# The mixture of LoRA experts of a four-block kernel, rewritten as a pipeline over tiles

## The chip, the cores and the metric

The kernel runs on one core of a Trainium2 chip. The time is device microseconds of that core for one execution. The text speaks of the engines as the profile does: PE is TensorE's matmul, PEld its weight load, DVE is VectorE, ACT is ScalarE, POOL is GpSimd, SP is SyncE, which here only starts DMAs.

## What is computed

The whole kernel is four blocks, each an attention-like mixer and a feed-forward part, on x of 16 x 128 x 256 in fp32. Only the last feed-forward part, a mixture of eight LoRA experts of rank 64, is changed. Of the reference, this part:

```python
def _L3_ffn_ref(x, A, B, Wr, br):          # x after layer norm
    x_flat = x.reshape(-1, d)
    logits = (x_flat @ Wr.T + br) / TEMPERATURE
    probs = jax.nn.softmax(logits, axis=-1)
    expert_idx = jnp.argmax(probs, axis=-1)
    expert_weight = jnp.max(probs, axis=-1)
    h = jnp.einsum('nd,erd->ner', x_flat, A)
    y = jnp.einsum('ner,eor->neo', h, B) * SCALING          # SCALING = 1/64
    sel = jnp.take_along_axis(y, expert_idx[:, None, None], axis=1)[:, 0, :]
    return sel * expert_weight[:, None]
...
x = x + jnp.tanh(g_ffn[3]) * _L3_ffn_ref(_layernorm(x, axis=-1), L3_ffn_A, L3_ffn_B, L3_ffn_Wr, L3_ffn_br)
```

The kernel doesn't gather: it computes the hidden row of all eight experts (512 numbers per token), multiplies it with a gate that is zero for seven of them, and takes the product with all of B.

## The kernel before, in words

A tile is one of the 16 blocks of 128 tokens (128 x 256); x lies in SBUF throughout, in four tensors xg[0..3] of GB = 4 tiles each, a group. The program is the function `passage`; it is followed by a second one under `tc.If`, which runs only when a flag says that a softmax sum left a safe range. In this execution it doesn't run. The flag is made by `verdict` (lines 66 to 80) from running extremes `inv`: four small DVE operations, a matmul with a column of ones (L76), three DVE operations on its result. All engines read the flag at the end (L48).

The stage ahead, `stage_l3x` (lines 1495 to 1801), is an attention whose order on PE, DVE and ACT is written out by hand (`tc.manual_schedule` over these three engines): instructions stay in the order in which the Python emits them. It ends, tile by tile, with `keep_values` (avs, L1704), `back` (ta, L1709), `normalise` (rc, inv, o: L1716, L63, L64, L1719), `turn` (tt, L1724), `keep_turned` (oT, L1729), `output` (y, L1735) and `store` (ys on ACT, L1740, and x on POOL, L1742).

The stage of the change is `stage_l3f` (lines 1804 to 1843). It is not under a manual schedule, so a scheduler orders its instructions; it also moved the group's layer norm statistics (`layernorm`, L155 to L160) of most groups into the attention. The loop runs over the four groups:
- layer norm of the group (xn, L163, with the power -0.5 on POOL, L160), `transposed` (L166 to L174: 8 transposes in two halves, copied out by DVE and ACT, L173), `logits` (L345, two fp32 matmuls of 8 columns a tile) and `exp_shifted` (L355).
- the gate: sum, reciprocal, `topk_mask` (L325 to L339, six DVE operations, four of them on 128 x 256 numbers) and three products (L1814 to L1819).
- for each tile of the group: ph = xn A (L1823, two fp32 matmuls with 512 columns), hid = ph times gate (L1831, DVE), four transposes of hid (L1835, tile tp), a copy to SBUF on ACT (hT, L1837), y = hid B (L1840, four fp32 matmuls with 256 columns), and x = x + tanh(g) y (L1842, DVE).
- one store of the group's four tiles, 512 KB (L1843, SP queue).

Each fp32 matmul shows in the trace as two passes, each with its weight load; a transpose is one. PSUM has two buffers for each of ph, y and tp. `verdict` is called between the two stages and has a PSUM pool of its own.

Other stages of the kernel (the shared expert of the first block, from line 516) are already written as pipelines in the manner that the change brings here; `stats` and `normal` of that stage (L593 to L605) are nearly the same functions.

Of the kernel before, what the change touches and what calls it, by code (L numbers as in the profile page):

```python
# [22 lines left out]
GB = 4  # L23
E = 8
I = 176
EI = E * I
LN_EPS = 1e-5
# [28 lines left out]
def passage(ctx: ExitStack, tc: tile.TileContext, a: dict, out: bass.AP, inv, flag):  # L56
    nc = tc.nc
    search = inv is None
# [4 lines left out]
            nc.vector.tensor_tensor(inv[:, 0, n], inv[:, 0, n], rc, ALU.max)  # L63
            nc.vector.tensor_tensor(inv[:, 1, n], inv[:, 1, n], rc, ALU.min)  # L64

    def verdict():

        with tc.tile_pool(name="vd", bufs=1) as vd, tc.tile_pool(name="vdp", bufs=1, space=PSUM) as ps:
            m = vd.tile([P, 2, 2], F32, name="m")
            nc.vector.tensor_reduce(m[:, 0], inv[:, 0], AX.X, ALU.max)  # L70
            nc.vector.tensor_reduce(m[:, 1], inv[:, 1], AX.X, ALU.min)
            nc.vector.tensor_scalar(m[:, 0], m[:, 0], 1e20, None, ALU.is_gt)
            nc.vector.tensor_scalar(m[:, 1], m[:, 1], 1e-30, None, ALU.is_lt)
            m = m.rearrange("p a b -> p (a b)")
# [16 lines left out]
    xg = [cst.tile([P, GB, D], F32, name=f"x{g}") for g in range(NG)]  # L91
# [15 lines left out]
    tri = consts[:, 7:71]  # L107
    sel = consts[0:2, 71:199]

    tg = cst.tile([P, 8], F32, name="tg")  # L110
# [4 lines left out]
    neghalf = cst.tile([P, GB], F32, name="neghalf")  # L115
# [33 lines left out]
    def layernorm(pool, g, extra=None, tag="xn"):  # L149

        x = xg[g]
        st = small.tile([P, GB, 6], F32, name="st")
        mv = small.tile([P, GB, 2], F32, name="mv")
        for k in range(GB):
            nc.vector.bn_stats(st[:, k, :], x[:, k, :])  # L155
            nc.vector.bn_aggr(mv[:, k, :], st[:, k, :])
        ve = small.tile([P, GB], F32, name="ve")
        nc.vector.tensor_scalar_add(ve, mv[:, :, 1], LN_EPS)
        rs = small.tile([P, GB], F32, name="rs")
        nc.gpsimd.tensor_tensor(rs, ve, neghalf, ALU.pow)  # L160
        xn = pool.tile([P, GB, D], F32, name="xn", tag=tag)
        for k in range(GB):
            nc.vector.tensor_scalar(xn[:, k, :], x[:, k, :], mv[:, k, 0:1], rs[:, k : k + 1], ALU.subtract, ALU.mult)  # L163
        return xn

    def transposed(pool, ps, xn, tag="xnT"):  # L166

        xT = pool.tile([P, 2, GB * P], F32, name="xnT", tag=tag)
        for c in range(2):
            t = ps.tile([P, GB * P], F32, name="tp", tag="tp")  # L170
            for k in range(GB):
                nc.tensor.transpose(t[:, k * P : (k + 1) * P], xn[:, k, c * P : (c + 1) * P], ident)
            (nc.scalar.copy if c else nc.vector.tensor_copy)(xT[:, c, :], t)  # L173
        return xT  # L174
# [35 lines left out]
    def stage_l0x(ka, vbuf, anyk):  # L210

        with tc.tile_pool(name="s0", bufs=1) as s0, tc.tile_pool(name="s0w", bufs=2) as s0w, tc.tile_pool(
# [103 lines left out]
            for b in range(0, B, 2):  # L316
# [3 lines left out]
                        nc.tensor.transpose(t[:, (2 * k + c) * P : (2 * k + c + 1) * P], oT[:, c, b + k, :], ident)  # L320
                xv = xg[b // GB][:, b % GB : b % GB + 2, :].rearrange("p b d -> p (b d)")
                nc.vector.scalar_tensor_tensor(xv, t, tg[:, 0:1], xv, ALU.mult, ALU.add)


    def topk_mask(v, k, pool):  # L325

        n = v.shape[1]
        mine, other = bc(v, 3, E), bc(v, 2, E)
        gt = pool.tile([P, n, E, E], F32, name="gt", bufs=1)
        nc.vector.tensor_tensor(gt, other, mine, ALU.is_gt)  # L330
        eq = pool.tile([P, n, E, E], F32, name="eq", bufs=1)
        nc.vector.tensor_tensor(eq, other, mine, ALU.is_equal)
        f = "p t a b -> p t (a b)"
        nc.vector.tensor_tensor(eq.rearrange(f), eq.rearrange(f), bc(tri, 1, n), ALU.mult)
        nc.vector.tensor_tensor(gt.rearrange(f), gt.rearrange(f), eq.rearrange(f), ALU.add)
        m = pool.tile([P, n, E], F32, name="m")
        nc.vector.tensor_reduce(m, gt, AX.X, ALU.add)
        nc.vector.tensor_scalar(m, m, k - 0.5, None, ALU.is_lt)
        return m  # L339

    def logits(ps, xT, gw, bias=None):
        lg = ps.tile([P, GB, E], F32, name="lg", tag="tp")
        for k in range(GB):
            for c in range(2):
                nc.tensor.matmul(  # L345
                    lg[:, k, :], lhsT=xT[:, c, k * P : (k + 1) * P], rhs=gw[:, c, :], start=(c == 0), stop=(c == 1)
                )
        l = small.tile([P, GB, E], F32, name="l")
        if bias is None:
            nc.vector.tensor_copy(l, lg)  # L350
        else:
            nc.vector.tensor_tensor(l, lg, bc(bias, 1, GB), ALU.add)
        return l

    def exp_shifted(l):  # L355

        mx = small.tile([P, GB], F32, name="mx")
        nc.vector.tensor_reduce(mx, l, AX.X, ALU.max)
        ex = small.tile([P, GB, E], F32, name="ex")
        nc.vector.tensor_tensor(ex, l, bc(mx, 2, E), ALU.subtract)  # L360
        nc.scalar.activation(ex, ex, AF.Exp)
        return ex


    def moe0_weights():
# [1436 lines left out]


    def stage_l3f(wa, wb, wr, br):
        with tc.tile_pool(name="lo", bufs=2) as lo, tc.tile_pool(name="lot", bufs=2, space=PSUM) as pst, tc.tile_pool(
            name="lou", bufs=2, space=PSUM
        ) as psu:
            for g in range(NG):
                xn = layernorm(lo, g)
                xT = transposed(lo, pst, xn)  # L1810
                ex = exp_shifted(logits(pst, xT, wr, br))

                s = small.tile([P, GB], F32, name="s")
                nc.vector.tensor_reduce(s, ex, AX.X, ALU.add)  # L1814
                nc.vector.reciprocal(s, s)
                gate = small.tile([P, GB, E], F32, name="gate")
                nc.vector.tensor_tensor(gate, ex, topk_mask(ex, 1, lo), ALU.mult)
                nc.vector.tensor_tensor(gate, gate, bc(s, 2, E), ALU.mult)
                nc.vector.tensor_scalar(gate, gate, 1.0 / 64.0, None, ALU.mult)  # L1819
                for k in range(GB):  # L1820
                    ph = psu.tile([P, E, 64], F32, name="ph")
                    for c in range(2):
                        nc.tensor.matmul(  # L1823
                            ph.rearrange("p e r -> p (e r)"),
                            lhsT=xT[:, c, k * P : (k + 1) * P],
                            rhs=wa[:, c, :],
                            start=(c == 0),
                            stop=(c == 1),
                        )
                    hid = lo.tile([P, E, 64], F32, name="hid")  # L1830
                    nc.vector.tensor_tensor(hid, ph, bc(gate[:, k, :], 2, 64), ALU.mult)  # L1831
                    t = pst.tile([P, 4, P], F32, name="tp")
                    hf = hid.rearrange("p e r -> p (e r)")
                    for i in range(4):
                        nc.tensor.transpose(t[:, i, :], hf[:, i * P : (i + 1) * P], ident)  # L1835
                    hT = lo.tile([P, 4, P], F32, name="hT")
                    nc.scalar.copy(hT, t)  # L1837
                    y = psu.tile([P, D], F32, name="y")
                    for i in range(4):
                        nc.tensor.matmul(y, lhsT=hT[:, i, :], rhs=wb[:, i, :], start=(i == 0), stop=(i == 3))  # L1840
                    xv = xg[g][:, k, :]
                    nc.vector.scalar_tensor_tensor(xv, y, tg[:, 7:8], xv, ALU.mult, ALU.add)  # L1842
                nc.sync.dma_start(out[g * GB : (g + 1) * GB].rearrange("b p d -> p b d"), xg[g])  # L1843

# [138 lines left out]
```

## Time and profile before

| what | us |
|---|---|
| median of 3 runs (1096.06 to 1099.82) | 1098.37 |
| the profiled execution | 1106.34 |
| its span, from the first to the last instruction | 1104.5 |
| first transpose of the stage starts | 999.66 |
| last x update of the stage ends | 1098.03 |
| mean granted TensorE clock of the span | 0.906 |

The profile is of one execution. A group of instructions is named by line, engine and operation, as out<-in by the tiles' names; busy matmuls overlap, so that their starts say more than their lengths. The granted clock is TensorE's, as a share of full speed. Of the whole span PE is busy 82%, DVE 56%, ACT 39%, POOL 33%; the stage of the change takes about the last tenth of it.

### The profile page before, as it was taken

The numbers are of one execution on the slowest core, as the hardware profiler recorded it, in microseconds if no ns is written. First come the engines' busy times: TensorE is split into PE (matmuls) and PEld (weight loads), VectorE is DVE, ScalarE is ACT, GpSimd is POOL, SyncE is SP. The second block draws the span as 40 slices with busy tenths as digits, with TensorE's granted clock in tenths as the row PEclk, the third lists the DMA queues.
The fourth block names the chain that finished last, engine by engine and source line by source line (L and its number), as shares of the span: only waits on it lengthen the run. The fifth ranks groups of instructions, "written<-read, shape, count | busy, mean of one in ns | idle before, by whom it ended". The sixth has DMA issues, their size and how long they took to land.

```text
span 1104.5 us, 14954 instructions
## 1 busy us (share of the span) xinstructions
PE 909.0 (82%) x5212; PEld 597.7 (54%) x5212; DVE 614.9 (56%) x1524; ACT 432.8 (39%) x658; POOL 365.9 (33%) x415
## 2 busy tenths in 40 slices
PE   3899888899999999966642858998179899998886
PEld 1444466677777454424422747887145555555563
DVE  5988947222225466349979677453445555545432
ACT  1211033232322444436750243455267677881110
POOL 5766222533024233045420136550533433200000
PEclk9999989999999999989985558899579999997999
DMA  9100080234313119000000202353589776610010
GB/s 304 34 0 0 3 232 1 77 100 108 70 58 124 34 39 187 1 0 1 1 1 0 77 1 77 115 146 85 154 230 252 199 209 191 174 44 1 20 39 22
DMA packets 71322, 94.12 MB, mean 85 GB/s; under 512 B 9191, under 2 KB 63047, under 8 KB 68935
## 3 DMA queue, kind: packets, MB, share of 16 engines
q1 hardware_dynamic: 56872, 67.21, 20.5%
q0 software_dynamic: 14080, 23.78, 10.8%
q10 hardware_dynamic: 288, 2.10, 0.5%
q8 instruction: 45, 0.74, 0.3%
q14 instruction: 37, 0.30, 0.1%
HBM read 57.06 MB, written 33.55 MB: 82 GB/s over the span
## 4 chain that ended last, share of the span: by engine, by line
PE 57%; DVE 21%; issue 8%; POOL 6%; ACT 5%; DMA 2%; another core or an unknown queue 0%; ACTq 0%; POOLq 0%; SPq 0%; DVEq 0%
PE y L307 8%; PE ub L674 4%; PE av L1693 3%; PE yb L700 3%; POOL yc L767 3%; PE s L1142 3%; PE y L1840 3%; PE s L1677 3%; PE yb L970 3%; PE av L1151 3%; PE up L535 2%; PE tq L1100 2%; DVE xn L163 2%; PE ph L1823 2%; DVE inp L489 1%
## 5 line engine op out<-in xcount | busy, mean ns | idle before, releaser
L1684 ACT ACTIVATE pt<-s 128x1024 f32<-128x1024 f32 x128 | 126.3, 1023 | 36.9 <-PE s L1677 34.4
L767 POOL DMA_INDIRECT yc<-ys,pos x64 | 62.0, 968 | 129.1 <-DVE x L786 55.2
L307 PE MATMUL y<-kv,toep 128*128 128x512 f32 x192 | 86.7, 603 | 1.1 <-DVE toep L247 1.1
L1677 PE MATMUL s<-qa,ka 64*128 64x256 f32 x512 | 64.3, 331 | 7.8 <-ACT pt L1684 7.0
L299 POOL TENSOR_TENSOR kv<-ctxT 128x1024 f32<-128x1024 f32 x32 | 60.1, 1899 | 28.5 <-PE y L307 28.5
L1693 PE MATMUL av<-pt,v 128*32 128x256 f32 x1024 | 69.4, 389 | 0.1
L1677 PEld LDWEIGHTS s<-qa,ka 64*128 64x128 f32 x512 | 38.5, 187 | 46.4 <-issue 22.9
L307 PEld LDWEIGHTS y<-kv,toep 128*128 128x128 f32 x192 | 35.6, 192 | 43.2 <-issue 39.8
L674 PE MATMUL ub<-L0we,xbT 128*128 x160 | 52.4, 472 | 2.6 <-ACT xbT L665 2.6
L651 POOL DMA_INDIRECT xb<-xs,who x40 | 38.1, 952 | 45.2 <-PE tb L663 34.2
L970 PE MATMUL yb<-L2we,hT 88*128 (+1 forms) x224 | 42.2, 318 | 8.3 <-DVE hT L794 4.0
L155 DVE BATCH_NORM_STATS2 st<-x 128x6 f32<-128x256 f32 x48 | 19.7, 415 | 52.3 <-POOL x L1742 39.8
L905 POOL DMA_INDIRECT xb<-xs,who x40 | 38.1, 952 | 30.4 <-PE tb L917 20.7
L1584 POOL TENSOR_TENSOR hl<-f,hl 128x512 fp32r<-128x512 f32 x16 | 20.5, 1281 | 77.9 <-ACT hl L1583 77.9
L312 DVE TENSOR_TENSOR pr<-y,qT 128x1024 f32<-128x1024 f32 x32 | 39.0, 1221 | 12.3 <-PE y L307 9.4
L1704 DVE COPY avs<-av 128x256 f32<-128x256 f32 x64 | 26.7, 417 | 30.9 <-PE av L1693 30.9
L535 PE MATMUL up<-L0s,xT 128*128 128x352 f32 x128 | 42.9, 480 | 0.0
L1145 ACT ACTIVATE pt<-s 128x1024 f32<-128x1024 f32 x32 | 32.7, 1023 | 25.4 <-PE s L1142 25.3
L970 PEld LDWEIGHTS yb<-L2we,hT 88*128 88x128 f32 x224 | 34.2, 208 | 15.1 <-DVE hT L794 8.5
L315 DVE TENSOR_REDUCE oT<-pr 128x128 f32<-128x1024 f32 x32 | 38.9, 1219 | 1.0
L674 PEld LDWEIGHTS ub<-L0we,xbT 128*128 128x128 f32 x160 | 29.7, 196 | 16.3 <-ACT xbT L665 2.8
L1693 PEld LDWEIGHTS av<-pt,v 128*32 128x32 f32 x1024 | 26.9, 110 | 20.4 <-issue 0.7
(380 smaller groups left out, 2061.7 us busy)
## 6 DMA issues: line engine op xcount, KB each, us to landing
scr<-hl SPq DMA_DIRECT2D x64, 256.0 KB
ys<-ysb SPq DMA_DIRECT2D x40, 256.0 KB
qa<-scr SPq DMA_DIRECT2D x32, 256.0 KB
ka<-scr SPq DMA_DIRECT2D x32, 256.0 KB
L2we<-in_L_w_dram POOLq DMA_DIRECT2D x6, 792.0 KB
L0we<-in_L_w_dram SPq DMA_DIRECT2D x6, 704.0 KB
xs<-xn SPq DMA_DIRECT2D x8, 512.0 KB
ctxT<-in_ctxT_dram ACTq DMA_DIRECT2D x2, 1024.0 KB
```

What stands on the lines that cost most here:

```text
L299: nc.gpsimd.tensor_tensor(t, bc(ch, 3, 8), bc(ch, 2, 8), ALU.mult)
L307: nc.tensor.matmul(y[:, ns], lhsT=T[:, h, d : d + P], rhs=kv[mc][:, ns], start=(mc == 0), stop=(mc == lc))
L312: nc.vector.tensor_tensor(pr, y.rearrange("p (b j i) -> p b j i", b=B, j=8), bc(qT[:, lc, :, hs], 2, 8), ALU.mult)
L315: nc.vector.tensor_reduce(oT[:, lc, :, hs], pr, AX.X, ALU.add)
L535: nc.tensor.matmul(t[:, n, 0 : 2 * I], lhsT=xT[:, c, b * P : (b + 1) * P], rhs=s13[:, c, n, :], start=(c == 0), stop=(c == 1),)
L651: nc.gpsimd.indirect_dma_start(out=xbs[s][:, i, :], out_offset=None, in_=xs, in_offset=bass.IndirectOffsetOnAxis(ap=who[:, 2 * s + i : 2 * ...
L674: nc.tensor.matmul(t[:, i, 0 : 2 * I], lhsT=xbT[:, i, c, :], rhs=we[:, bass.ds(regs[s][i] + c * 2 * I, 2 * I)], start=(c == 0), stop=(c == 1),
L767: nc.gpsimd.indirect_dma_start(out=got[b][:, i, :], out_offset=None, in_=ys, in_offset=bass.IndirectOffsetOnAxis(ap=pos[:, i, b : b + 1], ...
L970: nc.tensor.matmul(y[:, i, :], lhsT=hT[:, x, k, i, :], rhs=we[0:HI, bass.ds(at[i] + 4 * I + k * D, D)], start=(n == 0), stop=(n == 3),)
L1677: nc.tensor.matmul(s[:, h, jj, :], lhsT=ka[r, 2 * i + jj, sc * P : (sc + 1) * P], rhs=qa[r, 2 * i + jj, :], start=True, stop=True,)
L1684: nc.scalar.activation(pts[b, i][:, sc], s, AF.Exp)
L1693: nc.tensor.matmul(av[c : c + 32, :], lhsT=va[:, sc, 8 * h + 2 * i + jj, :], rhs=pt[:, sc, h, jj, :], start=(sc == 0), stop=(sc == 1),)
```

## The change

`stage_l3f` is put under a manual schedule on PE, DVE and ACT. Its work is cut into functions, and one loop over n emits, in each step, work of several tiles: the first product `up` of tile n, then the second product `down` of tile n-2, then `turn_hidden` (the transposes of hid) of tile n-1. Once a group, the transposes `turn` of the next group go ahead of these (n+2 a multiple of four) and its logits behind them (n+1 a multiple of four). Layer norm statistics run four tiles ahead, normalisation three. The gate is made otherwise: instead of comparing all pairs, the maximum of the exponentials is compared with each, and a running count (`tensor_tensor_scan`) keeps the first that is equal. Both halves of the transposed xn are copied out by ACT. PSUM gets one tag "a" with four buffers for the transposes, logits, th and y, and three for ph. The stores go out for two tiles at a time, and for the last two tiles singly. `verdict` is called in the step n = 4, with a tile of tag "a".

```diff
 
-    def verdict():
-
-        with tc.tile_pool(name="vd", bufs=1) as vd, tc.tile_pool(name="vdp", bufs=1, space=PSUM) as ps:
+    def verdict(ps):
+
+        with tc.tile_pool(name="vd", bufs=1) as vd:
             m = vd.tile([P, 2, 2], F32, name="m")
             nc.vector.tensor_reduce(m[:, 0], inv[:, 0], AX.X, ALU.max)
             nc.vector.tensor_reduce(m[:, 1], inv[:, 1], AX.X, ALU.min)
             nc.vector.tensor_scalar(m[:, 0], m[:, 0], 1e20, None, ALU.is_gt)
             nc.vector.tensor_scalar(m[:, 1], m[:, 1], 1e-30, None, ALU.is_lt)
             m = m.rearrange("p a b -> p (a b)")
-            t = ps.tile([1, 4], F32, name="t")
+            t = ps.tile([1, 4], F32, name="tv", tag="a")
             nc.tensor.matmul(t, lhsT=ones[:, 0:1], rhs=m, start=True, stop=True)
             f = vd.tile([1, 1], F32, name="f")
             nc.vector.tensor_reduce(f, t, AX.X, ALU.max)
...
-    def transposed(pool, ps, xn, tag="xnT"):
...
-    def topk_mask(v, k, pool):
...
-    def logits(ps, xT, gw, bias=None):
...
-    def exp_shifted(l):
...
     def stage_l3f(wa, wb, wr, br):
-        with tc.tile_pool(name="lo", bufs=2) as lo, tc.tile_pool(name="lot", bufs=2, space=PSUM) as pst, tc.tile_pool(
-            name="lou", bufs=2, space=PSUM
-        ) as psu:
-            for g in range(NG):
...
+        with tc.tile_pool(name="lo", bufs=2) as lo, tc.tile_pool(name="lot", bufs=4, space=PSUM) as pst, tc.tile_pool(
+            name="lou", bufs=3, space=PSUM
+        ) as psu, tc.manual_schedule(
+            engines={mybir.EngineType.PE, mybir.EngineType.DVE, mybir.EngineType.Activation}
+        ):
+            anew = lo.tile([P, GB, E], F32, name="anew", bufs=1)
+            nc.gpsimd.memset(anew, 1.0)
+            nc.gpsimd.memset(anew[:, :, 0:1], 0.0)
+            mvs, xns, xTs, lgs, gates, phs, hids, hTs, exs = [{} for _ in range(9)]
+
+            def stats(g):
+                mv = lo.tile([P, GB, 2], F32, name="mv")
+                st = lo.tile([P, GB, 6], F32, name="st")
+                    nc.vector.bn_stats(st[:, k, :], xg[g][:, k, :])
+                    nc.vector.bn_aggr(mv[:, k, :], st[:, k, :])
+                ve = lo.tile([P, GB], F32, name="ve")
+                nc.vector.tensor_scalar_add(ve, mv[:, :, 1], LN_EPS)
+                rs = lo.tile([P, GB], F32, name="rs")
+                nc.gpsimd.tensor_tensor(rs, ve, neghalf, ALU.pow)
+                mvs[g] = mv, rs
+
+            def normal(g):
+                mv, rs = mvs.pop(g)
+                xns[g] = xn = lo.tile([P, GB, D], F32, name="xn")
+                for k in range(GB):
+                    nc.vector.tensor_scalar(
+                        xn[:, k, :], xg[g][:, k, :], mv[:, k, 0:1], rs[:, k : k + 1], ALU.subtract, ALU.mult
+                    )
+
+            def turn(g):
+                xn = xns.pop(g)
+                xTs[g] = lo.tile([P, 2, GB * P], F32, name="xT")
+                for c in range(2):
+                    t = pst.tile([P, GB * P], F32, name="tx", tag="a")
+                    for k in range(GB):
+                        nc.tensor.transpose(t[:, k * P : (k + 1) * P], xn[:, k, c * P : (c + 1) * P], ident)
+                    nc.scalar.copy(xTs[g][:, c, :], t)
+
+            def logit(g):
+                lgs[g] = lg = pst.tile([P, GB, E], F32, name="lg", tag="a")
+                for k in range(GB):
+                            lg[:, k, :],
+                            lhsT=xTs[g][:, c, k * P : (k + 1) * P],
+                            rhs=wr[:, c, :],
+
+            def likely(g):
+                l = lo.tile([P, GB, E], F32, name="l")
+                nc.vector.tensor_tensor(l, lgs.pop(g), bc(br, 1, GB), ALU.add)
+                mx = lo.tile([P, GB], F32, name="mx")
+                nc.vector.tensor_reduce(mx, l, AX.X, ALU.max)
+                exs[g] = ex = lo.tile([P, GB, E], F32, name="ex")
+                nc.vector.tensor_tensor(ex, l, bc(mx, 2, E), ALU.subtract)
+                nc.scalar.activation(ex, ex, AF.Exp)
+
+            def chosen(g):
+
+                f = "p t e -> p (t e)"
+                ex = exs.pop(g)
+                s = lo.tile([P, 2, GB], F32, name="s")
+                nc.vector.tensor_reduce(s[:, 0], ex, AX.X, ALU.add)
+                nc.vector.tensor_reduce(s[:, 1], ex, AX.X, ALU.max)
+                nc.vector.reciprocal(s[:, 0], s[:, 0])
+                eq = lo.tile([P, GB, E], F32, name="eq")
+                nc.vector.tensor_tensor(eq, ex, bc(s[:, 1], 2, E), ALU.is_equal)
+                cum = lo.tile([P, GB, E], F32, name="cum")
+                nc.vector.tensor_tensor_scan(
+                    cum.rearrange(f), anew.rearrange(f), eq.rearrange(f), 0.0, ALU.mult, ALU.add
+                )
+                nc.vector.scalar_tensor_tensor(eq, cum, 1.0, eq, ALU.is_equal, ALU.mult)
+                nc.vector.tensor_tensor(ex, ex, eq, ALU.mult)
+                gates[g] = gate = lo.tile([P, GB, E], F32, name="gate")
+                nc.vector.scalar_tensor_tensor(gate, ex, 1.0 / 64.0, bc(s[:, 0], 2, E), ALU.mult, ALU.mult)
+
+            def up(b):
+                g, k = divmod(b, GB)
+                phs[b] = ph = psu.tile([P, E, 64], F32, name="ph", tag="u")
+                for c in range(2):
+                    nc.tensor.matmul(
+                        ph.rearrange("p e r -> p (e r)"),
+                        lhsT=xTs[g][:, c, k * P : (k + 1) * P],
+                        rhs=wa[:, c, :],
+                        start=(c == 0),
+                        stop=(c == 1),
+                    )
+
+            def gated(b):
+                g, k = divmod(b, GB)
+                hids[b] = lo.tile([P, E, 64], F32, name="hid")
+                nc.vector.tensor_tensor(hids[b], phs.pop(b), bc(gates[g][:, k, :], 2, 64), ALU.mult)
+
+            def turn_hidden(b):
+                hf = hids.pop(b).rearrange("p e r -> p (e r)")
+                t = pst.tile([P, 4, P], F32, name="th", tag="a")
+                for i in range(4):
+                    nc.tensor.transpose(t[:, i, :], hf[:, i * P : (i + 1) * P], ident)
+                hTs[b] = lo.tile([P, 4, P], F32, name="hT")
+                nc.scalar.copy(hTs[b], t)
+
+            def down(b):
+                g, k = divmod(b, GB)
+                hT = hTs.pop(b)
+                y = pst.tile([P, D], F32, name="y", tag="a")
+                for i in range(4):
+                    nc.tensor.matmul(y, lhsT=hT[:, i, :], rhs=wb[:, i, :], start=(i == 0), stop=(i == 3))
+                xv = xg[g][:, k, :]
+                nc.vector.scalar_tensor_tensor(xv, y, tg[:, 7:8], xv, ALU.mult, ALU.add)
+                if b >= B - 2:
+                    nc.sync.dma_start(out[b], xv)
+                elif k % 2:
+                    nc.sync.dma_start(out[b - 1 : b + 1].rearrange("b p d -> p b d"), xg[g][:, k - 1 : k + 1, :])
+
+            def when(f, b, n=B):
+                if 0 <= b < n:
+                    f(b)
+
+            for n in range(-4, B + 2):
+
+                def group(f, ahead):
+                    g, r = divmod(n + ahead, GB)
+                    if r == 0:
+                        when(f, g, NG)
+
+                group(turn, 2)
+                when(up, n)
+                when(down, n - 2)
+                when(turn_hidden, n - 1)
+                group(logit, 1)
+                group(likely, 1)
+                group(stats, 4)
+                group(normal, 3)
+                group(chosen, 0)
+                when(gated, n)
+                if n == GB and not search:
+                    verdict(pst)
...
         stage_l3x(*l3w, pos, wgt, ys)
-        if not search:
-            verdict()
         stage_l3f(l3a, l3B, l3r, l3br)
```

More of the change, by code (lines that the diff above doesn't have):

```diff
@@ L164, in layernorm @@
         return xn
-    def transposed(pool, ps, xn, tag="xnT"):
[L168 to L174, printed above, removed]
     def bc(ap, axis, n):
@@ L322, in stage_l0x @@
                 nc.vector.scalar_tensor_tensor(xv, t, tg[:, 0:1], xv, ALU.mult, ALU.add)
-    def topk_mask(v, k, pool):
[L327 to L339, printed above, removed]
-    def logits(ps, xT, gw, bias=None):
[L342 to L353, printed above, removed]
-    def exp_shifted(l):
[L357 to L362, printed above, removed]
     def moe0_weights():
@@ L1804, in stage_l3f @@
     def stage_l3f(wa, wb, wr, br):
-        with tc.tile_pool(name="lo", bufs=2) as lo, tc.tile_pool(name="lot", bufs=2, space=PSUM) as pst, tc.tile_pool(
-            name="lou", bufs=2, space=PSUM
-        ) as psu:
-            for g in range(NG):
[L1809 to L1819, printed above, removed]
-                for k in range(GB):
-                    ph = psu.tile([P, E, 64], F32, name="ph")
+        with tc.tile_pool(name="lo", bufs=2) as lo, tc.tile_pool(name="lot", bufs=4, space=PSUM) as pst, tc.tile_pool(
[10 more added lines that the diff above has]
+                st = lo.tile([P, GB, 6], F32, name="st")
+                for k in range(GB):
+                    nc.vector.bn_stats(st[:, k, :], xg[g][:, k, :])
[23 more added lines that the diff above has]
+                for k in range(GB):
@@ L1822, in stage_l3f @@
                     for c in range(2):
                         nc.tensor.matmul(
-                            ph.rearrange("p e r -> p (e r)"),
-                            lhsT=xT[:, c, k * P : (k + 1) * P],
-                            rhs=wa[:, c, :],
+                            lg[:, k, :],
+                            lhsT=xTs[g][:, c, k * P : (k + 1) * P],
+                            rhs=wr[:, c, :],
                             start=(c == 0),
@@ L1829, in stage_l3f @@
                         )
[L1830 to L1843, printed above, removed]
+            def likely(g):
[6 more added lines that the diff above has]
+                nc.scalar.activation(ex, ex, AF.Exp)
```

## The prediction

> **What bounds the kernel now.** The change touches only the last stage, so I read first where that stage lies and how full TensorE is in it: busy time by stretches, cut at the ends of the four groups. Columns: length, then busy time (count) of PE, PEld, DVE, ACT, POOL; granted clock; DMA.
>
> ```profile
> core 0: us, PE busy (x) PEld busy (x) DVE busy (x) ACT busy (x) POOL busy (x), PEclk, DMA share, GB/s
> 1003.00:1026.50 23.50, 22.29 (x85) 14.62 (x86) 9.82 (x33) 2.57 (x5) 1.02 (x1) 0.84 0.01 2
> 1026.50:1050.60 24.10, 20.70 (x90) 13.86 (x89) 10.16 (x27) 3.16 (x6) 0.00 (x0) 0.93 0.07 22
> 1050.60:1073.30 22.70, 19.30 (x90) 12.90 (x89) 8.80 (x23) 3.15 (x6) 0.00 (x0) 1.00 0.07 24
> 1073.30:1097.50 24.20, 20.38 (x84) 13.11 (x82) 8.10 (x22) 3.16 (x6) 0.00 (x0) 0.93 0.07 23
> 1097.50:1104.50 7.00, 0.01 (x1) 0.00 (x0) 0.48 (x1) 0.00 (x0) 0.00 (x0) 0.85 0.25 83
> ```
>
> PE looks 85 to 95% busy, so by this row about 12 us of the 94.5 could be won. [...] So I count starts instead, in a dense piece of the chain that ended last, together with the gate's chain ahead of it (start, us, what):
>
> ```profile
> 1053.58 0.20 DVE l L352
> ...
> 1057.51 0.19 DVE gate L1819
> ...
> 1057.80 0.70 DVE hid L1831
> ...
> 1058.55 0.66 PE tp L1835 x4
> 1059.20 0.86 PE ph L1823 x2
> 1060.06 1.86 PE y L1840 x8
> 1061.93 0.44 PE tp L1835 x4
> ```
>
> First, from the logits to the first hid each group spends 5 us on DVE, and PE runs dry. Second, the price of work: a tile has 4 passes of ph (64 over 16 tiles), 1.72 us, y 1.86, tp 0.44: 4.02 us. A group adds 8 transposes (0.88) and 16 logit passes (about 1.8). That makes 4 x 4.02 + 2.7 = 18.8 us a group, **75.1 us for the stage**. Before takes 98.4 us, from the first transpose (999.66) to the end of the last x (1098.03). By starts the ceiling is 23 us, not 12. Who takes it, by the waits of the stage (us in total, times, longest):
>
> ```profile
> PEld tp L1835 <- DVE hid L1831: 16.8, 8, 3.1
> PE tp L1835 <- DVE hid L1831: 10.1, 7, 2.3
> ```
>
> The rest is the clock. Short stretches catch its changes:
>
> ```profile
> 996.40:996.80 0.40, 0.12 (x1) 0.12 (x1) 0.40 (x4) 0.00 (x0) 0.00 (x0) 0.82 0.00 0
> 1010.00:1010.40 0.40, 0.40 (x2) 0.24 (x1) 0.36 (x4) 0.00 (x0) 0.16 (x1) 0.61 0.00 0
> 1034.00:1034.40 0.40, 0.00 (x0) 0.00 (x0) 0.40 (x2) 0.00 (x0) 0.00 (x0) 0.76 0.00 0
> 1085.20:1085.60 0.40, 0.40 (x3) 0.28 (x3) 0.00 (x0) 0.00 (x0) 0.00 (x0) 0.75 0.00 0
> ```
>
> It halves at 996.66 (0.82 is full clock for 0.26 of 0.40 us), is whole at 1010.31, halves at 1034.21, is whole (after another dip) at 1085.40[...]. Half clock costs 5.4 us at the start: transposes 1.95 for 0.88, logits 3.6 for 1.8, eight ph passes 5.94 for 3.44.
>
> **The change, part by part.** I take the instruction order of the changed kernel as built, which is fixed on PE, DVE and ACT. A slot is one step n of its loop: up(n), down(n-2), turn_hidden(n-1) on PE; s is its start.
>
> Start. The layer norm of group 0 now sits on DVE inside the drain of attention. Four bn_stats, four bn_aggr and ve, laid between rc, inv, o and oT. The pair ahead of each o pushes it back by 0.3 (0.09 + 0.32 of spacing less what waited anyway), so oT ends at 997.2 for 996.6, and the last bn_stats, bn_aggr and ve behind it (0.45 + 0.22 + 0.15) end near 997.9. The two memsets of anew are done by then on a POOL that is free from 992.7. The pow on POOL (1.02 by its row) follows, then xn, 999.1 against 998.67 before. The verdict that held DVE until 998.63 is gone from here, so these nearly cancel: transposes from about 999.8, 0.1 later. POOL's last addition to x waits behind that pow, but its reader, stats(3), comes only in slot 8. The slow clock stays, 5.4; so does the wait for ACT's copies, 0.7. th(0) no longer waits long; turn(1) waits 0.5 for normal(1).
>
> Gate chain. topk_mask with its 128x256 operations goes; eight 128x32 ones come, at 0.10 (independent) or 0.22 us (dependent, the l to ex spacing): 1.6 us. Its scan has no 128x32 row; the 128x128 one took 0.42, the 128x8 one 0.18, so 0.18 to 0.42, and I take 0.2. ACT now copies both halves of xT (0.58 each); it waits 61 us for tp in this stage and hides that.
>
> DVE in the slot of a group's first tile. stats comes in the same slot. How such alternation runs on DVE is shown by an earlier stage (timeline; start, us):
>
> ```profile
> 136.85 0.42 DVE L593 BATCH_NORM_STATS2 st<-x 128x6 f32<-128x256 f32 x1
> 137.30 0.18 DVE L594 BATCH_NORM_AGGREGATE mv<-st 128x2 f32<-128x6 f32 x1
> ...
> 139.10 0.17 DVE L596 TENSOR_SCALAR ve<-mv 128x4 f32<-128x4 f32 x1
> ```
>
> So stats takes 2.3 us. The slot's DVE row begins with the x update of tile n-2, which waits for its y: s + 3.8. Then 0.4 + 2.3 + 1.6 + 0.7 (hid) gives s + 8.8. PE wants that hid for its transposes at s + 4.02 + 3.58 = s + 7.6: a stall of 1.3 us, in slot 8 (slot 12 has no stats left, slot 0 is the start). In slots 5 and 9 the next group's xn stands behind an x update, and its transposes follow at once. If y ends at T, the fourth xn is there at T + 0.2 + 0.4 + 4 x 0.33 = T + 1.9 and four more transposes end at T + 2.45; unhindered they would at T + 0.44 + 0.88: 1.15 us in slot 5, and 0.8 in slot 9, where the x update runs beside th(8). In all other slots hid is ready 2 to 3 us early. PSUM doesn't stall: the four buffers of tag "a" are each read within two slots.
>
> The verdict. It moves into slot 4, and this is the dear part. Its ones-matmul stands on PE after turn_hidden(3), ahead of up(5). It waits for four reductions on DVE queued behind x update, stats(2), chosen(1) and hid(4): ready at s + 9.4, while PE is there at s + 4.0. PE is empty for **5.4 us**, with everything behind it: up(5), y(3), all later slots. DVE then waits in turn for that matmul, with x update 3, xn of group 2 and hid(5) behind it; PE is later still with y(3), so this adds nothing.
>
> Clock. [...] in 1030.79 to 1034.21 PE stood still for only 2.1 us (62%) and the clock fell. [...] I take 2.1. [...]
>
> End. The last tiles drain alone: PE waits twice for an hT copy (0.9 each), then x, 0.7. Only 128 KB instead of 512 KB then leave. Before, x ended at 1098.03 and the span at 1104.5; the transfer filled 1099 to 1101, and a quarter of it saves 1.4. Nine issues at 0.38 us instead of four, on an SP that waits for DVE, cost nothing.
>
> Sum: 75.1 + 5.4 + 0.7 + 0.5 + 5.4 (verdict) + 2.1 (clock) + 1.15 + 1.3 + 0.8 + 1.8 + 0.7 = 94.95 us against 98.4. Gain 3.45 - 0.1 (start) + 1.4 (end) = **4.8 us**. The pipeline itself would win more than 12; the verdict's place gives back 7.5. The profiled execution took 1106.34 (span 1104.5), 0.7% over the median of 1098.37, small enough to subtract from the median: **1093.6 us**.
>
> **Rivals.**
> - The verdict costs less: the clock is held or recovers at once, and DVE is a microsecond quicker. [...] 3.1 less: 1090.5.
> - The clock drops twice and recovers late (1.7 + 1.3): 1096.6, no measurable change. For: two of the last three groups dipped.
> - Slower: the verdict's gap halves the clock [...]. Each us of full-clock work costs one more; the gain is gone after 5 us of work beyond what I counted, slower by 0.3% after 8. Held for a group, 18.8 - 2.1 = 17 more: 1110. [...]
> - That the reordering isn't made is excluded by the order as built.
>
> **Numbers.** Forecast 0.50; cheap verdict 0.21; two drops 0.21; slower 0.08. About 0.3% (3.3 us) is what a measurement of this kernel can tell from no change, so the limit is 1095.1. The forecast's own spread (1092 to 1095.5) lies below it but for 0.05: faster 0.66, same 0.27, slower 0.07. Range 1088.5 to 1098.5.
>
> **What would show it.** Right: PE idle about 5 us ahead of the ones-matmul, released by DVE, and a clock of 0.5 after it; tiles 4.0 us apart elsewhere; short waits of tx for xn and of th(8) for hid; last x near 1094.6. Wrong: first transposes after 1000.5; tiles further apart than 4.2 us at full clock; clock below 1.0 after slot 7; the end after the last x not shorter than 6 us.

## The result, and the profile after

The changed kernel takes **1084.18 us** (median of 4, 1081.41 to 1086.45) beside 1098.36 (1096.06 to 1099.82): ratio **0.9872 [0.9843, 0.9901]**, 14.2 us. The forecast was 1093.6 (1088.5 to 1098.5): the right direction, a third of the size, and below the range.

The two profiled executions, cut at the same events. The first and the 15th of GpSimd's 16 additions to x (L1742 before, L1692 after) stand for the attention:

| piece, us | before | after | difference |
|---|---|---|---|
| start to first addition | 832.75 | 822.69 | -10.1 |
| first to 15th addition | 159.24 | 150.93 | **-8.3** |
| 15th addition to the end of the last av | 1.54 | 1.53 | 0 |
| last av to first logit | 8.79 | 8.45 | -0.3 |
| first logit to the end of the last x | 95.71 | 92.15 | -3.6 |
| last x to the end of the span | 6.47 | 6.35 | -0.1 |
| span | 1104.5 | 1082.1 | -22.4 |

The spans differ by 8.3 us more than the medians do, since the profiled execution of before lay 8.0 us above its median and that of after 0.35 below. This excess most likely lies in the first row and says nothing about the change: a later pair of profiles on another chip had the two first additions 3.4 us apart, with profiled runs 1.0 above and 2.0 below their medians. The last three rows give 4.0 us, close to the forecast's 4.8. **The 8.3 us in the attention, whose code the change doesn't touch, are what the forecast lacks.**

First that row. GpSimd's 1st, 9th and 15th addition before (start, us):

```profile
832.75 0.73 POOL L1742 TENSOR_TENSOR x<-x,ys 128x256 f32<-128x256 f32 x1
...
929.27 0.73 POOL L1742 TENSOR_TENSOR x<-x,ys 128x256 f32<-128x256 f32 x1
...
991.99 0.73 POOL L1742 TENSOR_TENSOR x<-x,ys 128x256 f32<-128x256 f32 x1 [8.87 <-ACT ys L1740]
```

and after:

```profile
822.69 0.72 POOL L1692 TENSOR_TENSOR x<-x,ys 128x256 f32<-128x256 f32 x1
...
910.93 0.73 POOL L1692 TENSOR_TENSOR x<-x,ys 128x256 f32<-128x256 f32 x1
...
973.62 0.73 POOL L1692 TENSOR_TENSOR x<-x,ys 128x256 f32<-128x256 f32 x1 [8.87 <-ACT ys L1690]
```

All of the 8.3 us lies ahead of the 9th addition (96.52 us for 88.24); from there to the 15th the two kernels take the same (62.72 and 62.69).

DVE's waits from 690 to 1000 us in the kernel before (waiter, what ended the wait: us in total, times, longest). Here st are the statistics of a tile, and avs is DVE's copy of the attention's product av:

```profile
DVE st L155 <- POOL x L1742: 39.8, 15, 4.0
DVE avs L1704 <- PE av L1693: 30.9, 39, 1.7
```

and in the changed kernel. There the statistics start only behind the last av product (975.61 us), and none waits for GpSimd:

```profile
DVE avs L1654 <- PE av L1643: 55.4, 53, 2.7
DVE xbT L744 <- ACT xbT L743: 27.2, 17, 1.7
DVE xn L1508 <- POOL rs L1502: 25.0, 13, 4.7
```

The last stage of before left DVE to the scheduler. It set each tile's bn_stats into DVE's order of work in the attention, behind GpSimd's addition to x and ahead of the next avs copy. There it holds up the copy: the products av of PE end at 867.65 and 869.64 us, their copies start at 871.11 and 872.04, behind the st that waits 3.98. DVE's timeline of before (start, us, instruction, idle before it and what ended that):

```profile
870.77 0.43 DVE L155 BATCH_NORM_STATS2 st<-x 128x6 f32<-128x256 f32 x1 [3.98 <-POOL x L1742]
871.11 0.41 DVE L1704 COPY avs<-av 128x256 f32<-128x256 f32 x1
...
872.04 0.42 DVE L1704 COPY avs<-av 128x256 f32<-128x256 f32 x1
```

PE pays, which is full there (busy for 87.15 of the 88.24 us in the changed kernel). Its waits over eight tiles, before (832 to 925 us), where s is the product of q and k, pt its exponentials, made by ACT, and ta the transposes of avs:

```profile
PE s L1677 <- ACT pt L1684: 3.8, 7, 0.6
PE ta L1709 <- DVE avs L1704: 2.3, 5, 1.0
```

and after (822 to 915 us):

```profile
PE ta L1659 <- DVE avs L1654: 0.7, 1, 0.7
```

These waits make 5.4 of the 8.3 us. Another 2.3 show as longer busy time of the same 916 matmuls (89.40 us for 87.15). Behind the 9th addition the statistics still wait for GpSimd, 14.8 of the 39.8 us, but there PE, just as full, shows no wait in either kernel, and nothing is lost.

Now the last stage. The stretches of after, cut near the starts of slots 4, 8 and 12 (columns as in the prediction):

```profile
983.60:1006.90 23.30, 23.04 (x94) 15.66 (x94) 9.26 (x33) 3.88 (x8) 1.02 (x1) 0.84 0.03 11
1006.90:1030.60 23.70, 18.12 (x76) 12.14 (x74) 9.31 (x35) 3.42 (x6) 1.01 (x1) 0.86 0.04 12
1030.60:1054.40 23.80, 22.64 (x99) 15.51 (x100) 10.15 (x36) 3.75 (x7) 1.01 (x1) 0.93 0.10 34
1054.40:1075.75 21.35, 19.37 (x83) 13.59 (x81) 7.19 (x19) 3.16 (x6) 0.00 (x0) 1.00 0.10 32
1075.75:1082.10 6.35, 0.00 (x0) 0.00 (x0) 0.00 (x1) 0.00 (x0) 0.00 (x0) 0.80 0.09 30
```

PE is 99 and 95% busy in the first and third stretch and still slow there: their mean granted clock is 0.84 and 0.93. It was 0.50 from 980.61 to 990.85, from 1011.33 to 1018.16 and from 1042.05 to 1045.46 us, and 1.00 otherwise up to the last x. The second stretch has the hole of the verdict. PE's waits from 990 us (tv is the verdict's ones-matmul, th the transposes of hid, tx those of xn):

```profile
PE tv L76 <- DVE m L73: 5.0, 1, 5.0
PE y L1866 <- ACT hT L1859: 1.5, 2, 0.7
PE th L1857 <- DVE hid L1851: 1.1, 1, 1.1
PE tx L1793 <- DVE xn L1783: 0.6, 1, 0.6
```

Of PE's waits of the hidden layer's transposes for hid, 10.1 us before, one of 1.1 us is left. PE's timeline at the verdict and near slot 9:

```profile
1013.37 0.19 PE L76 MATMUL tv<-m,ones 128*1 128x4 f32 x2 [5.03 <-DVE m L73]
1013.49 3.78 PE L1840 MATMUL ph<-l3a,xT 128*128 128x512 f32 x4
1017.07 2.43 PE L1866 MATMUL y<-l3B,hT 128*128 128x256 f32 x8
...
1040.12 0.66 PE L1857 MATMUL th<-ident,hid 128*128 128x128 f32 x4 [1.10 <-DVE hid L1851]
1040.84 2.12 PE L1793 MATMUL tx<-ident,xn 128*128 128x128 f32 x8
1042.75 3.23 PE L1840 MATMUL ph<-l3a,xT 128*128 128x512 f32 x4
1045.82 1.89 PE L1866 MATMUL y<-l3B,hT 128*128 128x256 f32 x8
...
1057.53 1.88 PE L1840 MATMUL ph<-l3a,xT 128*128 128x512 f32 x4
1059.25 1.89 PE L1866 MATMUL y<-l3B,hT 128*128 128x256 f32 x8
1060.98 0.60 PE L1857 MATMUL th<-ident,hid 128*128 128x128 f32 x4
1061.42 1.88 PE L1840 MATMUL ph<-l3a,xT 128*128 128x512 f32 x4
```

The first ph after each stall takes 3.78 and 3.23 us for 1.88, both at a granted clock of 0.50 for most of their length; slots without either are 1061.42 - 1057.53 = 3.89 us apart. The records overlap: the ph of 1057.53 ends at 1059.41, 0.16 us after the next y starts.

### The profile page after: what moved, and what is told of

The parts are those of the page before. It is cut to its first block, busy times and chain, and to the rows that moved or that the text cites. A ratio compares the mean times of both kernels' runs of the same rounds, so it can differ in the third digit from the quotient of the medians.

```text
span 1082.1 us, 14956 instructions
## 1 busy us (share of the span) xinstructions
PE 900.1 (83%) x5212; PEld 595.4 (55%) x5212; DVE 610.3 (56%) x1508; ACT 436.2 (40%) x662; POOL 366.3 (34%) x417
## 5 line engine op out<-in xcount | busy, mean ns | idle before, releaser
L920 PEld LDWEIGHTS yb<-L2we,hT 88*128 88x128 f32 x224 | 33.2, 202 | 13.2 <-DVE hT L744 10.1
L650 PE MATMUL yb<-L0we,hTb 88*128 x160 | 37.9, 379 | 0.0
```

The lines of the kernel that those rows point to most:

```text
L920: nc.tensor.matmul(y[:, i, :], lhsT=hT[:, x, k, i, :], rhs=we[0:HI, bass.ds(at[i] + 4 * I + k * D, D)], start=(n == 0), stop=(n == 3),)
```

## The experiments

Theory T: before, the statistics in DVE's queue cost the attention 8 us by waiting for GpSimd, and the rewritten stage took them out. Rival R: the attention's difference is scatter, and the stage gave more than its pieces show. For the stage itself: what do the verdict's place and the tail cost?

**1. The kernel before, with the statistics held back** by a copy that reads x of tile 14, ahead of them on DVE (edit shortened):

```
+ with tc.manual_schedule(engines={mybir.EngineType.DVE}):
+     fc = small.tile([P, 1], F32, name="fc")
+     nc.vector.tensor_copy(fc, extra)      # extra = xg[3][:, 2, 0:1]
      for k in range(GB):                   # bn_stats, bn_aggr
          ...
```

> The kernel before, with one edit: the layer norm statistics of the last stage are held behind the x of tile 14, so that none of them stands in VectorE's queue during the attention. Theory (a statistics instruction that waits for GpSimd's x holds up the avs copies behind it): the spacing of the x additions in the attention falls from 12.1 to 11.1 us, 8 us over the stage; the statistics then lie at the start of the last stage and give back 2 to 3, so 1092 to 1094 against 1098.4. Rival (the attention was shorter in the changed kernel by chance or by where its tiles lie in memory): spacing stays 12.1, time 1098 or later.

Measured: 1092.2 us, ratio 0.9947 [0.9935, 0.9959]. First to 15th addition 150.94 us (159.24 before), last av to last x 106.48 (104.50), as the statistics now come at the end. PE's waits from 825 to 918 us are those of the changed kernel:

```profile
PE ta L1719 <- DVE avs L1714: 0.7, 1, 0.7
```

T holds: without any change of the last stage's pipeline the attention gains 8.3 us, and 2 of it is given back.

**2. The changed kernel, with each tile's bn_stats back in the attention**, right behind the addition:

```
- ((store, -1), (stats, 4)),
+ ((store, -1), (stats, 4), (early, -1)),    # early: bn_stats of tile b - 1
```

> The changed kernel, with the bn_stats of each tile put back into the attention, behind the store of that tile. Theory: spacing 12.1 us again, 8 us lost in the attention; in the last stage the stall of th(8) (1.1 us) goes and the gap at the verdict shrinks by 2 us, so 1087 to 1090 against 1084.2. Rival (chance or placement): spacing stays 11.1, and only the gain in the last stage is seen, 1080 to 1082.

Measured: 1084.69 us, ratio 0.9877 [0.9859, 0.9896]. The wait is back on DVE,

```profile
DVE stE L1696 <- POOL x L1693: 41.5, 16, 4.0
DVE avs L1655 <- PE av L1644: 31.4, 39, 1.7
```

and the attention takes 158.25 us for 150.93, as T said; but the total doesn't rise, and there T's sum failed. What is lost comes back in the last stage: last av to last x is 92.87 us for 100.60. Its gaps shrink, since the slot has 0.5 us of statistics on DVE for 2.3:

```profile
1016.75 0.19 PE L76 MATMUL tv<-m,ones 128*1 128x4 f32 x2 [3.18 <-DVE m L73]
1016.87 2.52 PE L1846 MATMUL ph<-l3a,xT 128*128 128x512 f32 x4
1019.17 3.09 PE L1872 MATMUL y<-l3B,hT 128*128 128x256 f32 x8
```

The verdict's gap is 1.85 us shorter, the stall of th(8) and the half clock behind it are gone (2.4), and the first logits come 2.6 us sooner after the last av. So the change had two effects by one edit: statistics out of the attention (8.3 gained) and into the stage (7.7 paid).

**3. The same, one tile later**, when GpSimd has long added to x: `(early, -2)`.

> The changed kernel with the 16 bn_stats back in the attention as in the run before with early statistics, but each one tile (11 us) later, when GpSimd's addition to x is long done (the last tile's stays in the last stage). Theory: what the early statistics cost was the wait of DVE's queue for GpSimd, and nothing else: spacing of the additions in the attention 11.1 us as in the changed kernel (12.0 with the wait), no wait of a statistic for GpSimd. The last stage keeps what the early statistics gave it: from the first logit to the last x 86.5 us for 92.1, and the drain of the attention 3 us shorter. About 1075.5 us. Rival: early statistics cost their own time on DVE (16 x 0.6 us) and not the wait: spacing 11.8 to 12.0, about 1083 to 1085.

Measured: 1088.18 us on a chip on which the kernel before took 1104.67: ratio 0.9851 [0.98, 0.9902]. The expected time can't be set against this, since the kernel before is slower on this chip too. The stage came out: last av to last x 89.56 us, against 98.23 and 99.57 in two runs on such chips with the statistics in the stage (runs 8 and 7). The spacing didn't: 155.61 us in the attention are 11.7 a tile over the first eight, where T had 11.1 and the rival 11.8 or more. But those two runs, which have no statistics there, take as long (155.31, 155.65), so that statistics that wait for nobody cost nothing here. Why this is 155 and not 151 on these chips is taken up in run 8; on a chip with 151 this version was not run.

**4. The verdict in three pieces**: reductions at the end of slot 6, ones-matmul at the start of slot 7, the rest at its end.

```
+ if n == 7 and not search: next(vs)
  group(turn, 2)
  ...
- if n == GB and not search: verdict(pst)
+ if n == 6 and not search: vs = verdict(pst); next(vs)
+ if n == 7 and not search: next(vs, None)
```

> The changed kernel, with the verdict cut in three: its reductions at the end of slot 6, its matmul at the start of slot 7, the rest at the end of slot 7. Theory (the verdict's place costs 5.4 us of empty TensorE and 2 of half clock): both go, a stall of 1.3 us of th(4) for hid(4) appears: 6 us less, 1078. Rival (the gap is only shifted, the clock drops elsewhere): 2 us less or nothing, 1082 to 1084.

Measured: 1078.79 us, ratio 0.9827 [0.9814, 0.984]: 5.4 us below the changed kernel. PE's waits there, in the slowest of its five executions (1082.44 us):

```profile
PE th L1859 <- DVE hid L1853: 2.2, 2, 1.1
PE y L1868 <- ACT hT L1861: 1.5, 2, 0.7
PE tv L77 <- DVE m L73: 1.2, 1, 1.2
```

The 5.0 us have become 1.2, but th(4) now stalls as th(8) does, which the gap had hidden. By its pieces the stage gains 3.5 us (last av to last x 97.07 for 100.60), because both th stalls seem to be followed by a half clock here: behind the first, three of the four passes of ph take 2.77 us (1.88 for four at full clock), and from the start of th(4) to that of the last x it is 58.86 us, where run 5, with the same two stalls and no slow ph, has 53.87. Of these 5.0 us the wait for the ones-matmul makes 1.2; the rest is about twice the 1.70 that th(8) to the last x lost in the changed kernel against run 5 (35.15 for 33.45).

The same cut on top of run 3:

> The kernel of the run before this one (statistics in the attention one tile late) with the verdict cut in three over two slots as in the earlier split run. Theory: the 3.2 us that PE waits ahead of the ones-matmul there, and the half clock after it (1.4 us), go; no stall of th for hid is left in slots 4 and 8, since those slots have no statistics. 4 to 4.6 us less than without the cut: about 1071 us. Rival: PE then waits elsewhere for DVE, and only 2 us or less are gained: 1073 to 1075.

Measured: 1089.5 us, ratio 0.9848 [0.9805, 0.9891]; no gain that can be told from run 3. A miss, and the profiles say why. The gap does shrink, 3.18 to 1.22 us. But in run 3 no half clock had followed the gap (ph 1.98 us and y 1.89 behind it), and most of its first logits ran at full clock by their length,

```profile
997.08 1.73 PE L1807 MATMUL lg<-l3r,xT 128*128 128x8 f32 x14 [0.38 <-ACT xT L1801]
```

while in this run they took the 3.16 us that the same 14 take in the changed kernel at a granted clock of 0.50:

```profile
999.50 3.16 PE L1809 MATMUL lg<-l3r,xT 128*128 128x8 f32 x14 [0.17 <-ACT xT L1803]
```

That is 1.4 us, and last av to last x is 88.93 for 89.56. Whether half clock follows a stall differs from run to run of nearly the same work: behind 3.18 us it did in run 2 (ph 2.52 us, y 3.09) and not in run 3, behind 1.10 us it did in the changed kernel (ph 3.23) and not in run 5 (1.88).

**5. The verdict at its old place**, ahead of the stage's loop:

```
+ if not search: verdict(pst)
  for n in range(-4, B + 2):
  ...
- if n == GB and not search: verdict(pst)
```

> The changed kernel with the verdict called ahead of the stage's loop, where the kernel before has it, instead of in slot 4. Theory: the 5.0 us gap ahead of the ones-matmul and the 2.05 us of half clock after it go from the middle of the stage, but the first layer norm waits on DVE behind the verdict, which ends only with the last sums of the attention: the start is 2.5 to 4 us later. Net 3 to 4.5 us less: 1079.5 to 1081. Rival: the start isn't delayed at all, 1077; or the first normalisation is pushed behind everything, 7 us or more, and the place makes no difference: 1084.

Measured: 1092.38 us where before took 1104.67, ratio 0.9865 [0.9818, 0.9911]. Last av to last x 94.94 us for 98.23 to 100.60 with the verdict in slot 4. The start is later, as expected (PE waits 4.55 us for the first xn, first logit 11.10 us after the last av for 8.46), the middle 6 to 8 us shorter. So, by these pieces, moving the verdict into slot 4 cost the change 3.3 to 5.7 us net; the whole times can't show it, since the changed kernel wasn't timed on this chip.

**6. The tail.** The last four tiles stored by one 512 KB transfer, as before the change:

```
- if b >= B - 2: nc.sync.dma_start(out[b], xv)
- elif k % 2:
+ if b == B - 1: nc.sync.dma_start(out[b - 3 : b + 1]..., xg[g])
+ elif k % 2 and b < B - 4:
```

> The changed kernel, with the last four tiles stored by one DMA of 512 KB, as before. If the last transfer set the end, as the prediction had it, the stretch from the last x to the end of the span grows by 1.4 us from 6.35. If the jump over the second passage sets it (SyncE's branch of 3 us after the last issue), it stays within 0.2 us of 6.35.

Measured: one run of 1084.82 us; last x to the end 6.47 us for 6.35. The 512 KB land 3.6 us after their issue at 1076.65 (128 KB: 2.0 us), ahead of SP's next act at 1080.8. With four times the last transfer the end is 0.1 us later.

**7. The changed kernel without the flag's load and the conditional second passage** (which isn't executed here):

```
- again = nc.values_load(flag, ...)
- with tc.If(again != 0): passage(tc, a, out, None, None)
```

> The changed kernel without the flag's load and without the branch and the second passage behind it, which is not executed in this run anyway (so it leaves out what would happen if the verdict asked for a second passage). Theory: the time from the end of the last x to the end of the span, 6.35 us, is set by the jump over the second passage's code (3.1 us on SP between its branch and its next event) and the flag's load (0.5): 2.3 to 3 us remain, about 1080.5 us. Rival: the last output transfer sets the end: the tail stays at 5.5 us or more, about 1083.5 us.

Measured: 2.98 us from the last x to the end, for 6.35. The one run took 1092.79 us, on the slower chip, and can't be set against 1084.18. So 3.4 us of the tail belong to the flag's load and the jump, which this run leaves out together. The trace gives most of them to the jump: SP's and DVE's rows of the branch's line in the changed kernel (duration ns min/median/max, first and last start):

```profile
L51 SPq EVENT_SEMAPHORE  x8: 17/17/17, 1079.9 to 1080.4; - x8
...
L51 DVEq COMPARE_BRANCH  x1: 72/72/72, 1075.9 to 1075.9; - x1
...
L51 SPq COMPARE_BRANCH  x1: 45/45/45, 1076.8 to 1076.8; - x1
L51 DVEq EVENT_SEMAPHORE  x1: 21/21/21, 1079.2 to 1079.2; - x1
```

PE, DVE, ACT and SP are silent for 3.1 to 3.5 us after their branches (GpSimd, which branches 35 us earlier, at 1038.7, for 2.6). SP branches at 1076.8 and next acts at 1079.9; the 128 KB have landed by then (2.0 us after their issue at 1075.78).

**8. Both kernels again, on one further chip, and the best version.** The best version has the statistics of run 3, the cut verdict with its ones-matmul behind `down`, and `normal` ahead of it:

```
  when(up, n)
+ group(normal, 3)
  when(down, n - 2)
+ if n == 7 and not search: next(vs)
  when(turn_hidden, n - 1)
- group(normal, 3)                 # stood behind stats
```

> The changed kernel itself, unaltered, so that it stands on one chip beside the version below and beside a profile of the kernel before. On the chip of the last four runs the kernel before took 1104.7 us for 1098.1, and four kernels showed 155.6 us from the first to the fifteenth addition to x in the attention where the same attention had shown 150.9 on the others. Theory: the gain of the change itself is the same everywhere, 13 to 15 us below the kernel before, if the chip is like the first ones. Rival: the attention's gain depends on the chip, and a chip with 155.6 us there shows a gain of 8 to 9 us.

> The kernel before, unaltered, for its profile on the same chip as the two other runs. Theory: its 16 statistics in the attention wait 4 us each for GpSimd wherever it runs: 159 us from the first to the fifteenth addition to x, 8 more than the changed kernel beside it, and 104 us from the last av product to the last x (100.6 for the changed kernel). Rival: on a chip where the changed kernel takes 155.6 us there, the kernel before takes the same 159, so that only 3.5 us are between them.

> The changed kernel with the statistics in the attention one tile late, the verdict cut in three with its ones-matmul behind the second product of slot 7, and each group's normalisation ahead of that slot's update of x. Theory: the 1.2 us ahead of the ones-matmul and the three waits of the transposes for xn (1.5 us in sum) go, and no stall is left that halves the clock after the start: 80 us from the first logit to the last x, for 92.1 in the changed kernel and 82.6 to 83.1 in the two runs with late statistics; 12 to 14 us below the changed kernel on the same chip, about 1071. Rival: the waits return at another place (the normalisation ahead of the x update delays hid), 83 us or more.

Measured on that chip: before 1106.84 us, changed 1096.01 (ratio 0.9915 [0.9887, 0.9942]), **best version 1084.14 (0.9805 [0.9784, 0.9826])**, 11.9 us below the changed kernel (12 to 14 expected). From the first logit to the last x it takes 79.13 us (expected 80), for 89.77 in the changed kernel beside it and 92.15 in its first profile. PE's waits from 985 us are down to these:

```profile
PE y L1875 <- ACT hT L1868: 1.5, 2, 0.7
PE tx L1802 <- DVE xn L1792: 0.9, 2, 0.8
PE tt L1677 <- DVE o L1672: 0.5, 1, 0.5
```

The first expectation's rival is right that the change's gain depends on the chip: 10.8 us here, between its 8 to 9 and the theory's 13 to 15. Before takes 159.24 us in the attention on both chips with a profile of it, the changed kernel 150.93 on one and 155.31 on the other. PE's waits over eight tiles (830 to 924 us) of the changed kernel there:

```profile
PE s L1627 <- ACT pt L1634: 3.9, 7, 0.6
PE ta L1659 <- DVE avs L1654: 0.6, 1, 0.6
```

Of the two rows of before, the one for avs is gone here as well; the one for pt, seven times 0.6 us, is not. It is absent in the first profile of the changed kernel and in runs 1, 2, 4 and 6 (one chip), and present in all seven kernels profiled on the two later chips. Where it is present, ACT stands idle for 1.0 to 1.1 us ahead of one pt in most tiles, and starts it 0.5 us after PE's record of its s has ended (0.1 us elsewhere). What holds it up the runs don't show, and why it went away with the statistics on the first chips but not on the later ones stays open.

## Why the prediction was wrong, and where it was right

**The step that failed is its first sentence: "The change touches only the last stage".** The diff does; the program didn't. The kernel before gave DVE's order in that stage to a scheduler, which had drawn bn_stats of finished tiles into the attention, where each but the last waited 1.4 to 4 us for GpSimd and held the avs copies behind it. That they stood there is told ahead of the prediction; the prediction costed them as 2.3 us added to a slot and put what they cost at their old place at nothing. Eight of those 15 waits cost PE about 1 us each. Runs 1 and 2 show the two halves of it: 8.3 us gained in the attention by moving nothing but them, 7.3 lost there by putting them back. On the chip of run 8 the attention gains 3.9.

Point by point, by the prediction's steps:

- Work floor, 4.02 us a tile: 3.89 measured. Right, though the difference makes 2.1 us over 16 tiles.
- Start, transposes 0.1 later than before: from the end of the last av to the first of them 6.29 us for 6.13. Right. Half clock through the first logits and ph: right here (0.50 from 980.61 to 990.85 us; 14 logit passes take 3.16 us, eight of ph 5.38); in run 3 the logits took 1.73.
- Scan: 0.23 us by its row (0.2 taken). th(8): 1.10 on PE (1.3; the prediction's own terms, 8.8 less 7.6, give 1.2). Slots 5 and 9: ph starts 1.3 us late after each (1.15 and 0.8), the second partly through the clock.
- Verdict: 5.03 us (5.4), and 2.3 for the clock after it (from the start of ph to that of th 5.85 us, for 3.55 in run 3 at the same place). The 2.1 that the prediction takes for the clock was its author's estimate; no trace of before shows it. Both fit. Run 5 prices the place at 3.3 to 5.7 net.
- A clock drop near slot 9, left to a rival (1.7 in "the clock drops twice"): it came in the first profile (granted clock 0.50 from 1042.05 to 1045.46 us; from ph to y 3.07 us for 1.72, 1.35 lost), but by the lengths of ph (1.88 us) not in the second (run 8) nor in run 5, whose stalls of th are the same 1.1 us. Standstill ahead of it doesn't tell. The prediction has a drop behind 2.1 us of standstill in 3.42. In the 3.41 us ahead of this one (1038.64 to 1042.05 us) PE was busy for 2.25 us, 1.88 of them with transposes, and stood still for 1.16. In the kernel before, a stretch of 3.42 us with only 1.54 us of busy PE, all of it ph (1054.68 to 1058.10), was followed by no drop: the granted clock was 1.00 up to 1081.99. What decides it isn't shown.
- End, 1.4 us for the smaller transfer: wrong. The tail shrank by 0.1; runs 6 and 7 show that the flag's load and the jump over the unexecuted passage set it, and that the transfer lies beneath. The prediction named this test ("the end after the last x not shorter than 6 us"), and the sign of being wrong came; so did "clock below 1.0 after slot 7", with the drop at 1042.05 us.
- Sum of the stage, from the first transpose to the last x: 94.95 predicted, 94.3 measured. That it fits to 1% is in part luck: the floor was 2.1 us lower and the drop near slot 9, not in the sum, cost 1.35; the second profile of the same kernel has 91.9. The forecast missed by 9.4 us: 8.3 of attention outside its view, 0.6 more gained in stage and start, 1.3 less in the tail, and 1.8 that remain of the table's first row once the excess of the profiled runs over their medians is taken off.
- Rivals: "clock drops twice" happened in the first profile and was hidden by the 8.3 us; the verdict was not cheap (5.03 + 2.3 us of the 7.5 forecast); "slower" had no part.

## What to carry to other kernels

When a stage leaves a scheduler's hands for a written order, compare every engine's order over the whole program: what the scheduler had drawn into other stages goes away there. An instruction on a path that is full should stand where its slowest source is already done: the same statistics cost 7.3 us right behind the addition they wait for, and nothing that shows one tile later, on a chip whose attention a further wait held at 155 us. Such a wait cost time here only where another engine then waited for the held-up work: behind the last seven of the 15 (14.8 us), PE did not. And a step that is called once (a verdict, a check) belongs where no chain waits; cut it so that each engine's share sits behind work it would do anyway.

## What the hardware showed that I had not expected

- Behind the branch over the second passage, PE, DVE, ACT and SP were silent for 3.1 to 3.5 us in the changed kernel (SP 1076.8 to 1079.9; PE's branch 3.37 us by its row, 3.47 before the change). Leaving it and the flag's load out shortens the end from 6.35 to 2.98 us. On SP these 3.1 us are the largest single item after the last output; the flag's load takes 0.54.
- Half clock followed some stalls and not others: gaps of 5.0 us were followed by it in both profiles of the changed kernel (ph 3.78 and 3.46 us for 1.88), one of 3.18 us in run 2 (ph 2.52, y 3.09; 1.7 us lost) and not in run 3 (1.98, 1.89), th stalls of 1.1 us probably twice in run 4 (above) and never in run 5 (ph 1.88 both times). What decides it these runs don't show. The stage of one and the same kernel differed by 2.4 us between two profiles (100.60 and 98.23).
- In the changed kernel PE's waits for pt, seven of 0.6 us in the attention, were there on one chip and not on another: 4 us of 1090 that no difference of code explains.
